# The last pair's expert results, summed by products with a matrix of weights at tokens instead of through memory

## The chip, the cores and the metric

The kernel runs on one core of a Trainium2 chip. The metric is the device time of one execution in microseconds (us); a time stated for a kernel is the median of its runs. The profile shows one execution, with its own time. Engines are named as in the profile: PE is TensorE (PEld its weight loads), DVE is VectorE, ACT is ScalarE, POOL is GpSimd, SP is SyncE, which here only issues DMAs.

## The reference, cut to what matters

A model of four layers on x, 4 x 256 tokens of 256 numbers, f32. Each layer adds an attention step and a feed-forward step to x. The change touches only the last one, a mixture of 64 experts of which each token uses 8:

```python
def _L3_ffn_ref(hidden_states, gate_w, gate_proj_w, up_proj_w, down_proj_w):
    B, S, H, I, E, K = (2, 128, 256, 96, 64, 8)      # run on the 1024 normed tokens
    x = hidden_states.reshape(-1, h)
    router_logits = x @ gate_w
    routing_weights, selected = jax.lax.top_k(router_logits, K)
    routing_weights = jax.nn.softmax(routing_weights, axis=-1)
    ...
    gate = jax.lax.ragged_dot(hidden_sorted, gate_proj_w, group_sizes)
    up = jax.lax.ragged_dot(hidden_sorted, up_proj_w, group_sizes)
    down = jax.lax.ragged_dot(jax.nn.silu(gate) * up, down_proj_w, group_sizes)
    out = down[unsort].reshape(-1, K, h)
    out = jnp.sum(out * routing_weights[..., None], axis=1)
...
x = x + _L3_ffn_ref(_layernorm(x, axis=-1), ...)
```

So each token's output is x plus a weighted sum of eight experts' results.

## The kernel before, in words

**Names.** P = 128 partitions, D = 256, NT = 8 tiles of 128 tokens (`x_t(t)` is tile t of x, kept on the chip), K3 = 8 choices of a token, E3 = 64 experts, CAP = 192 rows for each expert, S = 256. `ident` is the 128 x 128 identity, `kpos` holds 0 to 255 along each row. A token's eight choices are numbered in the order of their experts: choice 0 is its expert with the lowest number, choice 7 the one with the highest. `choice_w[:, t, j]` is the weight of choice j for the tokens of tile t.

**Scatter.** While the third layer's attention ends, GpSimd writes the normed row of each token eight times to `hs`, a buffer in HBM with 192 rows for each expert (L1702). Each row is HW = 257 wide; its last element is the number 8 * token + choice of the place where its result belongs. Rows that stay empty carry NPAIR = 8192 there, one beyond the end. `yd`, in HBM too, has a row for each of these 8192 places and is filled with zeros early in the kernel.

**The expert loop** (`experts`, L2040) takes two experts at a time, in 32 pairs, numbered 0 to 31. For a pair p, whose 384 rows stand in `hbs[p]` as three groups j of 128 rows: TensorE turns the rows (`rows_turned`, L1892), ScalarE copies them back (L1900), TensorE makes the gate sums (L2055) and the up sums (L1986), ScalarE the gate's silu (L2059), VectorE two products (L2071, L1991), TensorE the results of 384 rows (L1999, L2004), and ScalarE copies these over the pair's rows in `hbs[p]` (L2083). Then `put_results(p)` has GpSimd write them to `yd` by three indirect DMAs, one for each group of 128 rows (L2009), to the places that the rows carry. The iteration for pair p+1 does the results of pair p. At its end `beside(p)` places what else runs: the choice weights of a tile in even pairs below 16, two diagonal matrices a pair from pair 16 on (`diag[:, t // 2, j, :]` is `ident` times the weight of choice j, for the even tiles t; L2025), the rows of pair p + 7 (`load_rows`, L443), weights of later experts (L416), the loads of `load_results`, and four early adds (L1939).

The order on TensorE, VectorE, ScalarE, GpSimd and SyncE is the program's order (`tc.manual_schedule`): a waiting instruction holds up what stands behind it on its engine. Waits follow from what an instruction reads and writes; the loads of `load_results` wait for just those puts that can hold their choices (`needs`, L421).

**Loads of results.** Since choices stand in the order of experts, the rows of choice j are complete in `yd` after a certain pair. `LOADS` groups the choices (0 and 1, 2, 3, 4, 5, 6 and 7) and L1952 computes the pair: 23, 27, 28, 29, 30 and 31. `load_results(js, p)` (L1908, L1927) then loads these choices of all tokens back to the chip, 1 MB for a choice, in one DMA, in two halves, or for 6 and 7 in four parts, all on SyncE's queue; `result(t, j)` is the part for tile t.

**The sums** (`sums`, L2094) follow the last pair. For the even tiles TensorE adds up the choices in PSUM, by products of `diag` with `result` (`sum_result`, L1944), choice by choice over the four tiles: choices 0 to 5 first, then 6 and 7 tile by tile; VectorE adds x (L1779). For the odd tiles VectorE does all: x plus weight times result, one operation for each choice (`add_result`, L1939), behind a marker on GpSimd (`tick`, L2101) that stands after its last put. ScalarE's queue issues the eight stores (L2096).

## Time and profile before

| what | value |
|---|---|
| median of 10 runs | 642.79 us (642.0 to 644.01) |
| the profiled execution: time / span | 643.89 us / 642.2 us |
| busy PE / PEld / DVE / ACT / POOL, us | 590.6 / 449.9 / 423.9 / 373.8 / 403.3 |
| mean granted TensorE clock | 0.971 |
| chain that ended last, by engine | PE 44%; POOL 18%; issue 12%; DVE 10%; ACT 8%; DMA 5% |
| puts to `yd` (L2009) | x84 shown with hb as source, 1001 ns mean |
| sums on TensorE (L1944) | from 618.22 to 638.73 us of the span |

How to read it: times inside the execution are us from the start of its span, which is 1.7 us shorter than its time. A line of a table of stretches gives, for each engine, busy time and the number of instructions, then the granted clock (1.00 is full speed), the busy share of the DMA engines and GB/s. In a timeline a line has start, length, engine, line of the kernel, operation, output<-inputs and a count of records; what stands in brackets is idle time before it and what ended that. TensorE's matmuls are pipelined, so the distance from one to the next counts, not the length of a record. A few records can be missing from a trace.

### The profile page before, as it was taken

To read this page: it belongs to the slowest core of one execution; us is meant where nothing else is said; L and a number is where in the kernel's file an instruction comes from. 1 tells how busy PE (TensorE), PEld (TensorE's weight loads), DVE (VectorE), ACT (ScalarE), POOL (GpSimd) and SP (SyncE) were. 2 spreads that over 40 slices of the span, in tenths; PEclk is the share of its full clock that TensorE was granted. 3 is DMA by queue.
4 is the path that set the end of the run, shared out by engine and by line. 5 is a ranking of instruction groups with operands and counts; after the bars stand their busy time and mean duration, and the time that the engine had idled before them with its cause. 6 is when DMAs were issued, how large, how long until landed. Compare 5 with 4: busy or idle time off the path is not lost.

```text
span 642.2 us, 10891 instructions
## 1 busy us (share of the span) xinstructions
PE 590.6 (92%) x3727; PEld 449.9 (70%) x3740; DVE 423.9 (66%) x1063; ACT 373.8 (58%) x900; POOL 403.3 (63%) x532
## 2 busy tenths in 40 slices
PE   5997799998999999999999989999839999999995
PEld 4773347686688777877877867886627887778873
DVE  5678947878687789669988766485534555433437
ACT  2233337868988976456886768579444454545420
POOL 6997898213627543664735885787773777676660
PEclk9997979999999999999999989999959999999998
DMA  8999999920210023000003111053458978979687
GB/s 283 365 387 239 193 198 176 301 61 26 83 33 3 1 66 115 2 0 1 1 2 98 42 67 58 34 187 108 159 150 281 300 239 276 305 229 304 212 265 263
DMA packets 66305, 98.13 MB, mean 153 GB/s; under 512 B 7206, under 2 KB 54007, under 8 KB 66240
## 3 DMA queue, kind: packets, MB, share of 16 engines
q1 hardware_dynamic: 56320, 78.40, 43.0%
q0 software_dynamic: 7680, 16.84, 7.4%
q10 hardware_dynamic: 2240, 2.10, 1.0%
q8 instruction: 32, 0.52, 0.4%
q14 instruction: 33, 0.27, 0.1%
HBM read 58.42 MB, written 43.07 MB: 158 GB/s over the span
## 4 chain that ended last, share of the span: by engine, by line
PE 44%; POOL 18%; issue 12%; DVE 10%; ACT 8%; DMA 5%; POOLq 1%; SPq 1%; DVEq 0%; ACTq 0%
POOL yd L2009 10%; PE ps_q L1519 5%; PE ps_y L1623 3%; POOL hs L1702 3%; PE ps_g L1120 3%; PE ps_u L1120 2%; PE ps_y L1402 2%; DMA hs<-hx,slots 2%; PE ps_u L1604 2%; DMA hb<-hs 2%; PE ps_p L742 2%; PE ps_s L1380 2%; PE tp_q L1277 2%; PE ps_s L1554 1%; PE tp_e L1588 1%
## 5 line engine op out<-in xcount | busy, mean ns | idle before, releaser
L2009 POOL DMA_INDIRECT yd<-hb x84 | 84.1, 1001 | 34.2 <-issue 20.4
L1702 POOL DMA_INDIRECT hs<-hx,slots x64 | 65.7, 1026 | 24.2 <-issue 13.0
L903 POOL TENSOR_TENSOR st<-st,mhalf 128x1 f32<-128x1 f32 x56 | 33.0, 593 | 56.4 <-DVE st L899 44.2
L1566 ACT ACTIVATE e<-ps_s,nm 128x128 f32<-128x128 f32 x128 | 45.8, 412 | 5.6 <-DVE nm L1560 5.5
L1991 DVE TENSOR_TENSOR act<-ps_u,g 64x192 f32<-64x192 f32 x64 | 22.7, 354 | 39.7 <-PE ps_u L1986 39.3
L2083 ACT COPY hb<-ps_y 128x768 f32<-128x768 f32 x27 | 21.6, 800 | 36.5 <-PE ps_y L2004 36.5
L2071 DVE TENSOR_TENSOR act<-ps_gu,g 32x384 f32<-32x384 f32 x32 | 18.0, 562 | 33.8 <-ACT g L2059 33.5
L1478 POOL TENSOR_TENSOR hh<-g,v 128x512 f32<-128x512 f32 x16 | 20.2, 1274 | 23.8 <-ACT g L1476 19.9
L1281 ACT ACTIVATE qT<-tp_q,rnd 128x512 bf16<-128x512 f32 (+2 forms) x48 | 25.7, 567 | 10.8 <-PE tp_q L1277 10.7
L1566 ACT ACTIVATION_READ_ACCUMULATOR e<-ps_s,nm 128x1 f32 x128 | 31.2, 251 | 0.0
L1533 POOL TENSOR_TENSOR deep<-rt 64x512 f32<-64x512 f32 x20 | 27.0, 1348 | 5.9 <-DVE rt L1529 2.7
L1519 PE MATMUL ps_q<-qc,deep 96*128 96x256 f32 x128 | 30.4, 380 | 0.0
L1185 ACT ACTIVATE e<-ps_s,nb 128x256 f32<-128x256 f32 x64 | 30.1, 493 | 0.0
L906 DVE TENSOR_SCALAR h<-x,st 128x256 f32<-128x256 f32 x56 | 26.7, 488 | 5.1 <-POOL st L903 4.8
L1623 PE MATMUL ps_y<-bo,u 128*128 128x256 f32 x128 | 29.3, 381 | 0.1
L2059 ACT ACTIVATE g<-ps_gu 96x384 f32<-96x384 f32 x32 | 15.6, 486 | 23.2 <-PE ps_gu L2055 23.2
L1900 ACT COPY hbT<-tp_hb 128x768 f32<-128x768 f32 x31 | 24.7, 798 | 6.9 <-PE tp_hb L1892 5.1
L1120 PE MATMUL ps_g<-hT,w_gate 128*128 128x512 bf16 x69 | 21.0, 447 | 8.0 <-ACT hT L1100 4.3
L1529 DVE TENSOR_TENSOR rt<-ps_q,rope 128x512 f32<-128x512 f32 x32 | 20.9, 684 | 9.4 <-PE ps_q L1519 9.4
L1583 DVE TENSOR_TENSOR e<-e,nm 128x512 f32<-128x512 f32 x32 | 25.8, 806 | 1.3
L1519 PEld LDWEIGHTS ps_q<-qc,deep 96*128 96x128 f32 x128 | 24.1, 190 | 3.5 <-ACT qc L1505 0.3
L1623 PEld LDWEIGHTS ps_y<-bo,u 128*128 128x128 f32 x128 | 23.6, 190 | 3.4 <-ACT u L1608 0.5
(373 smaller groups left out, 1777.3 us busy)
## 6 DMA issues: line engine op xcount, KB each, us to landing
hs<-order SPq DMA_DIRECT2D x1, 12336.0 KB, 95.2
hb<-hs SPq DMA_DIRECT2D x28, 385.5 KB, 5.7
yd<-order SPq DMA_DIRECT2D x1, 8192.0 KB, 30.6
deep<-in_w_gu SPq DMA_DIRECT2D x8, 768.0 KB, 6.4
wt<-in_w_gu SPq DMA_DIRECT2D x6, 768.0 KB, 6.0
deep<-in_w_dn SPq DMA_DIRECT2D x8, 384.0 KB, 6.2
wt<-yd SPq DMA_DIRECT2D x3, 1024.0 KB, 7.3
wt<-in_w_dn SPq DMA_DIRECT2D x6, 384.0 KB, 8.5
```

The costliest lines, as they stand in the source:

```text
L903: nc.gpsimd.tensor_tensor(s[:, 8:9], s[:, 7:8], mhalf, ALU.pow)
L906: nc.vector.tensor_scalar(h[:, k, :], x_t(t), ss[k][:, 6:7], ss[k][:, 8:9], ALU.subtract, ALU.mult)
L1120: nc.tensor.matmul(ps.ap, w[:, dc, o : o + P], q[:, dc, :], start=k == 0, stop=k == n - 1)
L1185: nc.scalar.activation(e[:, mt, :], s[:, mt, :], AF.Exp, bias=nb[:, mt : mt + 1], accum_out=tot[:, 2 * j + mt : 2 * j + mt + 1],)
L1281: nc.scalar.activation(qT[:, 4 * i : 4 * i + full, :], tp.ap[:, :full, :], AF.Identity, bias=rnd[:, 1:2])
L1519: nc.tensor.matmul(ps.ap[:, k, :], w[:, hp * P : (hp + 1) * P], qc.ap, start=True, stop=True)
L1533: nc.gpsimd.tensor_add(qv(q[i])[r, hps, :], t0[r], t1[r])
L1566: nc.scalar.activation(wide[:, k, :], s.ap[:, k, :], AF.Exp, bias=nm[:, k : k + 1], accum_out=tot[:, k : k + 1],)
L1583: nc.vector.tensor_mul(wide, wide, tot.unsqueeze(2).to_broadcast([P, n, nk * P]))
L1623: nc.tensor.matmul(y.ap, u[:, hp, :], bo3[:, hp, :], start=hp == 0, stop=hp == H3 // 2 - 1)
L1702: put = nc.gpsimd.indirect_dma_start(out=hs[:, :], out_offset=bass.IndirectOffsetOnAxis(ap=slots[:, t, j : j + 1], axis=0), in_=rows[:, j, ...
L2009: put = nc.gpsimd.indirect_dma_start(out=yd[:, :], out_offset=bass.IndirectOffsetOnAxis(ap=hbs[p][:, j, D : D + 1].bitcast(I32), axis=0), ...
```

## The change

The rows of the last pair (31) are not written to `yd` any more. Each of the pair's three groups of 128 rows gets, for each of four blocks of 256 tokens, a matrix of 128 rows by 256 tokens that holds the row's weight in the column of its token and zero elsewhere (`own_part`, twelve in all, on old buffers and four new ones). In the sums TensorE multiplies these with the results that still stand in `hbs[31]`. In `yd` the places of these rows keep their zeros, so the other sums add nothing for them, and all choices can be loaded after pair 30 at the latest. Every tile, odd ones too, now has its own sum in PSUM, which starts with x (`sum_x`, a product with the identity) or with the last pair's part (`sum_own`). Choices 4 and 5 of odd tiles are scaled by ScalarE in place and added by products with the identity (`sum_scaled`); choices 0 to 3 of odd tiles are added to x by VectorE as before, choices 6 and 7 by VectorE on the sum. ScalarE copies the even tiles' sums to x; the odd tiles' stores go to SyncE's queue.

In the loop, `own_rows` (pair 2) loads the places that the last pair's rows carry; `own_tokens` (pair 15) works out the tokens and writes `choice_w` to a new HBM buffer `wd`; `own_weights` (pairs 16, 20, 24) gathers the rows' weights from it by an indirect DMA each; `own_places` (pairs 18 to 29, one matrix a pair) makes the matrices.

The diff, cut to its core:

```diff
+    wd = dram.tile([NPAIR, 1], F32, tag="wd", name="wd")
...
+    part_of = [moe_tile([P, S], f"own{k}", 1) for k in range(4)] + [dsc0, b2o]
+    part_of += [
+        q.bitcast(F32)[:, k * S : (k + 1) * S]
+        for q in (q12, q1_both.rearrange("p k i -> p (k i)")[:, : 2 * RPP * HW]) for k in range(RPP)
+    ]
+    own_i, own, own_w = (moe_tile([P, RPP], n, 1) for n in ("own_i", "own", "own_w"))
+    own_from = moe_tile([P, NT * P // S, RPP], "own_from", 1)
...
+    last = n_pairs - 1
+    def own_rows():
+        ld = nc.sync.dma_start(
+            own_i.bitcast(I32),
+            hs[2 * last * CAP :, D : D + 1].bitcast(I32).rearrange("(j p) o -> p (j o)", p=P),
+        )
+        needs(ld, "put", [i for js in puts for i in js], "rows of all choices")
+    def own_tokens():
+        nc.vector.tensor_copy(own, own_i.bitcast(I32))
+        nc.vector.tensor_scalar(own, own, 1.0 / K3, 0.5 / K3 - 0.5, ALU.mult, ALU.add)
+        nc.vector.tensor_scalar(own, own, ROUND, ROUND, ALU.add, ALU.subtract)
+        for k in range(NT * P // S):
+            nc.vector.tensor_scalar(own_from[:, k], own, float(k * S), None, ALU.subtract)
+        nc.vector.memset(own_w, 0.0)
+        nc.sync.dma_start(wd[:, :].rearrange("(t p j) o -> p t (j o)", p=P, j=K3), choice_w)
+    def own_weights(j):
+        nc.gpsimd.indirect_dma_start(
+            out=own_w[:, j : j + 1], out_offset=None, in_=wd[:, :],
+            in_offset=bass.IndirectOffsetOnAxis(ap=own_i[:, j : j + 1].bitcast(I32), axis=0),
+            bounds_check=NPAIR - 1, oob_is_err=False,
+        )
+    def own_part(j, k):
+        return part_of[j * (NT * P // S) + k]
+    def own_places(j, k):
+        nc.vector.tensor_scalar(
+            own_part(j, k), kpos, own_from[:, k, j : j + 1], own_w[:, j : j + 1], ALU.is_equal, ALU.mult
+        )
...
-            y, diag[:, t // 2, j, :], result(t, j), start=j == 0, stop=j == K3 - 1
+        nc.tensor.matmul(y, diag[:, t // 2, j, :], result(t, j), start=False, stop=j == K3 - 1)
+    def sum_x(y, t):
+        nc.tensor.matmul(y, ident, x_t(t), start=t % 2 == 0, stop=False)
+    def sum_scaled(y, t, j):
+        nc.tensor.matmul(y, ident, result(t, j), start=False, stop=j == K3 - 3)
+    def sum_own(y, t):
+        for j in (0, 2, 1):
+            k, o = divmod(t * P, S)
+            nc.tensor.matmul(
+                y, own_part(j, k)[:, o : o + P], hbs[last][:, j, :D], start=t % 2 == 1 and j == 0, stop=False
+            )
     for js in LOADS:
-        last = max(min(BOUND[j] - 1, E3 - K3 + j) // 2 for j in js)
-        loaded[last] = js
+        p = max(min(BOUND[j] - 1, E3 - K3 + j, E3 - 3) // 2 for j in js)
+        loaded.setdefault(p, []).append(js)
...
-        if p in loaded:
-            load_results(loaded[p], p)
+        for js in loaded.get(p, ()):
+            load_results(js, p)
+        if p == FIRST:
+            own_rows()
+        if p == 2 * NT - 1:
+            own_tokens()
+        if p in own_at:
+            own_weights(own_at[p])
+        if 0 <= p - own_first - 2 < RPP * NT * P // S:
+            own_places(*divmod(p - own_first - 2, NT * P // S))
         if p in added_at:
             add_result(*added_at[p])
+    own_first = 2 * NT
+    own_at = {own_first + j * NT * P // S: j for j in range(RPP)}
...
                     nc.scalar.copy(yb[:, 1, :], y[:, 1])
+                    beside(p - 1)
+                    break
                 put_results(p - 1, yb)
...
     def sums():
-        ys = {t: (ps_mm if t < NT // 2 else ps_acc)([P, D], "ps_sum") for t in range(0, NT, 2)}
+        first = [ps_mm([P, D], "ps_sum") for _ in range(2)]
+        second = [ps_acc([P, 4, D], "ps_sums") for _ in range(2)]
+        ys = (
+            first[0], tp_rows[:, 0, :D], first[1], tp_rows[:, 1, :D],
+            second[0][:, 0], second[0][:, 2], second[1][:, 0], second[1][:, 2],
+        )
+        evens, odds = range(0, NT, 2), range(1, NT, 2)
         put_out = nc.gpsimd.memset(tick, 0.0)
-        for j in range(K3 - 2):
-            for t in range(0, NT, 2):
+        for t, j in on_dve[EARLY_ADDS : -NT]:
+            if j < K3 - 4:
+                add = add_result(t, j)
...
+        def known_sums(t):
+            sum_x(ys[t], t)
+            for j in range(K3 - 4):
                 sum_result(ys[t], t, j)
-        for t, j in on_dve[EARLY_ADDS : -NT]:
-            add = add_result(t, j)
...
-        for t in range(0, NT, 2):
-            for j in range(K3 - 2, K3):
+        for t in evens[:-1]:
+            known_sums(t)
+        for t in range(NT - 2):
+            sum_own(ys[t], t)
+        known_sums(NT - 2)
+        for t in (NT - 2, NT - 1):
+            sum_own(ys[t], t)
+        for t in odds:
+            sum_x(ys[t], t)
+        for j in (K3 - 4, K3 - 3):
+            for t in odds:
+                nc.scalar.activation(
+                    result(t, j), result(t, j), AF.Copy, scale=choice_w[:, t, j : j + 1]
+                )
+            for t in evens:
                 sum_result(ys[t], t, j)
-                add_result(t + 1, j)
-            store(t + 1)
-            add_to_x(t, ys[t])
-            store(t)
+            for t in odds:
+                sum_scaled(ys[t], t, j)
+        for t in evens:
+            for j in (K3 - 2, K3 - 1):
+                sum_result(ys[t], t, j)
+            nc.scalar.copy(x_t(t), ys[t])
+            store(nc.scalar, t)
+            for j, v in ((K3 - 2, ys[t + 1]), (K3 - 1, x_t(t + 1))):
+                nc.vector.scalar_tensor_tensor(
+                    x_t(t + 1), result(t + 1, j), choice_w[:, t + 1, j : j + 1], v, ALU.mult, ALU.add
+                )
+            store(nc.sync, t + 1)
```

More of the change, by code (lines that the diff above doesn't have):

```diff
@@ L1943, in sum_result @@
     def sum_result(y, t, j):
-        nc.tensor.matmul(
-            y, diag[:, t // 2, j, :], result(t, j), start=j == 0, stop=j == K3 - 1
-        )
+        nc.tensor.matmul(y, diag[:, t // 2, j, :], result(t, j), start=False, stop=j == K3 - 1)
[9 more added lines that the diff above has]
+            )
     loaded = {}
     for js in LOADS:
-        last = max(min(BOUND[j] - 1, E3 - K3 + j) // 2 for j in js)
-        loaded[last] = js
+        p = max(min(BOUND[j] - 1, E3 - K3 + j, E3 - 3) // 2 for j in js)
+        loaded.setdefault(p, []).append(js)
     on_pe = [(t, j) for j in range(K3) for t in range(0, NT, 2)]
@@ L2094, in sums @@
     def sums():
-        def store(t):
-            nc.scalar.dma_start(out[t // 2, t % 2 * P : (t % 2 + 1) * P, :], x_t(t))
-        ys = {t: (ps_mm if t < NT // 2 else ps_acc)([P, D], "ps_sum") for t in range(0, NT, 2)}
-        put_out = nc.gpsimd.memset(tick, 0.0)
-        for j in range(K3 - 2):
-            for t in range(0, NT, 2):
-                sum_result(ys[t], t, j)
-        for t, j in on_dve[EARLY_ADDS : -NT]:
-            add = add_result(t, j)
-            tc.add_manual_dep(
-                add.ins, put_out.ins.name,
-                mybir.DependencyInfo(mybir.DependencyClass.Sync, mybir.DependencyReason.DATA),
-                reason="the last results are on their way",
-            )
@@ L2112, in sums, with store @@
-        for t in range(0, NT, 2):
-            for j in range(K3 - 2, K3):
-                sum_result(ys[t], t, j)
-                add_result(t + 1, j)
-            store(t + 1)
-            add_to_x(t, ys[t])
-            store(t)
+        def store(queue, t):
+            queue.dma_start(out[t // 2, t % 2 * P : (t % 2 + 1) * P, :], x_t(t))
+        first = [ps_mm([P, D], "ps_sum") for _ in range(2)]
[4 more added lines that the diff above has]
+        )
@@ new lines, in sums @@
+        evens, odds = range(0, NT, 2), range(1, NT, 2)
+        put_out = nc.gpsimd.memset(tick, 0.0)
+        for t, j in on_dve[EARLY_ADDS : -NT]:
+            if j < K3 - 4:
+                add = add_result(t, j)
+                tc.add_manual_dep(
+                    add.ins, put_out.ins.name,
+                    mybir.DependencyInfo(mybir.DependencyClass.Sync, mybir.DependencyReason.DATA),
+                    reason="the last results are on their way",
+                )
+        def known_sums(t):
+            sum_x(ys[t], t)
+            for j in range(K3 - 4):
+                sum_result(ys[t], t, j)
@@ L2120, in model @@
+        for t in evens:
[6 more added lines that the diff above has]
+                    x_t(t + 1), result(t + 1, j), choice_w[:, t + 1, j : j + 1], v, ALU.mult, ALU.add
+                )
+            store(nc.sync, t + 1)
     with tc.manual_schedule(engines=ORDERED | {mybir.EngineType.SP}):
```

## The prediction

> **What bounds the kernel now.** The change touches the expert loop and the sums behind it, so I first read the table of stretches (width, then busy time of each engine with its instructions, granted clock, DMA share, GB/s):

> ```profile
> core 0: us, PE busy (x) PEld busy (x) DVE busy (x) ACT busy (x) POOL busy (x), PEclk, DMA share, GB/s
> ...
> 580.00:600.00 20.00, 20.00 (x143) 15.69 (x141) 8.23 (x25) 9.82 (x15) 13.81 (x15) 1.00 0.82 268
> 600.00:610.00 10.00, 10.00 (x73) 8.24 (x72) 4.28 (x14) 4.87 (x8) 6.80 (x7) 1.00 0.59 211
> 610.00:620.00 10.00, 9.17 (x57) 6.42 (x56) 4.41 (x14) 3.84 (x6) 7.17 (x8) 1.00 0.72 214
> 620.00:630.00 10.00, 7.76 (x34) 6.21 (x34) 5.42 (x14) 0.00 (x0) 3.63 (x5) 0.98 0.95 314
> ```

> The loop is bound by TensorE (20.00 of 20.00 us); from 620 on TensorE idles and the DMA is full. Second, the chain that ended last, from 600 us on:

> ```profile
> 623.51 3.33 DMA yd<-hb
> ...
> 626.96 6.63 DMA cx<-yd
> ...
> 638.83 0.36 DVE x L1779
> ```

> The end hangs on the last pair's puts, on their landing, and on the load of choices 6 and 7 behind them. This is the chain that the change cuts. Third, what TensorE does meanwhile (start, length, line; xN are records):

> ```profile
> 618.22 1.13 PE L1944 MATMUL ps_sum<-deep,diag 128*128 128x256 f32 x4
> ...
> 620.92 4.48 PE L1944 MATMUL ps_sum<-wt,diag 128*128 128x256 f32 x20
> 625.23 1.03 PE L1944 MATMUL ps_sum<-q,diag 128*128 128x256 f32 x4
> 626.54 1.13 PE L1944 MATMUL ps_sum<-q,diag 128*128 128x256 f32 x4 [0.28 <-DMA q<-yd]
> 629.63 2.08 PE L1944 MATMUL ps_sum<-q,diag 128*128 128x256 f32 x4 [1.96 <-DMA q<-yd]
> ...
> 636.32 2.41 PE L1944 MATMUL ps_sum<-ctxT,diag 128*128 128x256 f32 x8 [0.21 <-DMA ctxT<-yd]
> ```

> The page for L1944 adds up to 64 records (24+12+8+8+8+4), and sum_result is called 32 times (8 choices, 4 even tiles): one f32 product of 128x128 by 128x256 is two records. From 620.92 to 625.23 stand 20 records, 10 products: **0.431 us a product**. The whole stage of 32 needs 13.8 us of TensorE and lies in a window of 20.5 us (618.22 to 638.73); 6.7 us are waits and low clock. That 6.7 us is all the cover there is for new products.

> **The change part by part.** The page's execution has a span of 642.2 us and a time of 643.89; the median of the ten runs is 642.79. I work out a difference of spans and add it to the median.

> 1. Products in the sums. By the diff: known_sums on four even tiles, 4 x (1 + 4) = 20; sum_own on eight tiles, 8 x 3 = 24; sum_x on four odd tiles, 4; choices 4 and 5, 2 x (4 + 4) = 16; choices 6 and 7 of the even tiles, 8. That is **72 products in place of 32**, all of the one shape, in one written order on TensorE. 72 x 0.431 = 31.0 us. Started at 618.22 like today and never waiting, they end at 649.25 instead of 638.73: +10.5 us. No row prices them lower: 379 ns is a record's length in the pipeline, 0.2155 us its pitch, and the slow rows are slower (0.81 us a product at half clock, the 1.62 us of weight loads for wmask). The cover of 6.7 us is counted in this difference already.

> 2. The new order makes a wait. Today choice 3 is first read by the 13th product (618.22 + 12 x 0.438 = 623.5). Now known_sums(0) reads it in the fifth, at 618.22 + 4 x 0.431 = 619.95. Its load, by the source line of the loads:

> ```profile
> L1927 SPq DMA_DIRECT2D wt<-yd x1: 360/360/360, 616.5 to 616.5; - x1
> ...
> DMA to landing us min/median/max: 5.8/5.8/5.8
> ```

> It is issued at 616.5, when pair 28's puts have landed, and lands at 622.3 in the full DMA stretch. The diff moves neither its pair (28) nor what runs beside it. TensorE waits from 619.95 to 622.3: **+2.35 us**, with all 68 other products queued behind it. Were it to land after the 4.0 us of this line's shortest load, at 620.5, the wait would be 0.5; after 9.2, the longest, 5.75. I take its own row.

> 3. The clock after that wait. Three stretches of 3.41 us, one on each side of the clock's fall and one with a smaller gap:

> ```profile
> 626.12:629.53 3.41, 1.27 (x5) 0.68 (x4) 3.41 (x10) 0.00 (x0) 0.00 (x0) 1.00 0.84 255
> 629.53:632.94 3.41, 3.31 (x8) 2.53 (x8) 3.06 (x8) 0.00 (x0) 0.00 (x0) 0.50 0.94 297
> 165.32:168.73 3.41, 2.08 (x15) 1.53 (x15) 2.37 (x7) 3.30 (x6) 3.24 (x5) 1.00 0.57 175
> ```

> With TensorE busy 1.27 of 3.41 us the clock falls to 0.50 for the next 3.41 us; with 2.08 of 3.41 it does not. A wait of 2.35 us inside one such stretch leaves 1.06 us busy, fewer than the 1.27 that fell. If the fall comes, half of 3.41 us is lost: **+1.7 us**. Whether the stretch contains the wait depends on where it begins. With the limit midway (1.7 us idle), the wait is split too evenly to matter in 1.05 of 3.41 positions; so about 7 in 10 that it falls (9 in 10 and 5 in 10 at the two ends of the bracket). I take the fall. [...]

> 4. After the products. Today 3.47 us lie between the last product's end (638.73) and the span's end: an add of 0.42, a store of 2.4 and the close. Now it is a copy on ScalarE (0.37, as L2088) and a store behind it: the same 3.5 us. ScalarE needs about 0.8 us for each tile (0.37 and an issue of 0.38, median), TensorE 0.86, so it keeps up; were each issue the longest shown, 0.93, it would end about 1 us later. VectorE's two operations for each odd tile (2 x 0.48) are done before the last even tile's.

> 5. Loads, puts, adds. Choices 6 and 7 are asked for behind choice 5, at about 625.6 instead of 626.96; 3 MB at the 330 to 390 GB/s of these stretches land by 634 to 636. TensorE reaches choice 5 after 60 products, beyond 645, and choice 6 later: no wait, and nothing gained, since TensorE is last. The three puts of pair 31 (3 x 1.28 us) go, off TensorE's path. VectorE's twelve adds start near 620.7 (behind the third put at 619.68) and need 5.5 us; sum_x of the odd tiles, product 45, comes after 640. The eight scalings on ScalarE (0.49 at most, from L1185) take 3.9 us between landing and use.

> 6. Inside the loop (4.255 us a pair). Twelve own_places, one a pair from 18 to 29: 0.488 us each by L906 (same size, two scalars per partition). VectorE idles 1.32 us before L2071 in these pairs, 0.92 where an early add stands: hidden, with 0.4 us or more left. Uncovered, 5.9 us. Eight small operations in pair 15 (8 x 0.154 by L899) meet 1.72 us of idle. Three gathers on POOL at the 1.28 us pitch of a put: POOL has 4.255 - 3 x 1.275 = 0.43 us free a pair, so each is worked off in three pairs, before the next, and the rows behind are loaded seven pairs ahead. own_rows and the write of wd go on SP's queue, which waits there for puts already. The one wait that can reach TensorE: own_places stands in VectorE's order before L2071, and waits for its gather. From the gather's issue (about 595.8 for the third, after the put at 594.54) to that place two pairs later (600.1, after the diag operations) are 4.3 us, plus 0.8 of idle. Indirect writes land in 2.3 to 6.7 us in these stretches; the first gather also waits for wd, whose 1024 rows of 32 bytes no row prices. Each may cost 0 to 1.6 us: 0 to 5 in all. I take 0, since the median landings at the first two places are 2.3 to 3.4. [...]

> Sum: 10.5 + 2.35 + 1.7 = 14.6 us; span about 656.8, median **657.4 us**.

> **The rivals.**
> (a) Faster: the two records of a product are not the pitch I take them for, and a product costs 0.2155 us. Then 68 of them end at 622.3 + 14.7 = 637.0, the shorter DMA chain (choices 6 and 7 1.3 us sooner) shows, and the median is about 641. It decides only where a product costs under 0.22 us. For it stands the chain, where the DMA is last; against it the 64 records for 32 calls. 3%; no measurable change, 1%.
> (b) No wait for choice 3 (it lands before 620): the products alone, 653.3. 8%.
> (c) The wait, but the clock stays: 655.7. 26%.
> (d) My forecast, wait and clock: 657.4. 44%.
> (e) The forecast and a loss in the loop, from the gathers or a VectorE operation not covered: 1 to 4 us, 658.4 to 661.4. 18%.

> **How the numbers follow.** A measurement of this kernel tells about 0.2% (1.3 us) from no change. Faster is (a), 3%; within it 1%; slower is the rest, 96%. The range reaches from just below (b) to most of (e): 653.0 to 660.8.

> **What would show it.** In the profile after: 144 records under the four lines of the sums in place of 64, back to back up to about 653; the last loads landed some 15 us before TensorE's end; a wait of about 2.3 us on wt<-yd near 620, and half clock in the 3.4 us behind it; TensorE, not POOL and DMA, on the chain's last 30 us; the loop's pairs still 4.255 us. I am wrong if products come closer than 0.43 us, if TensorE still idles behind 623, or if L2071 comes late in pairs 18, 22 and 26.

## The result, and the profile after

The changed kernel takes **657.82 us** (median of 13 runs, 655.22 to 661.77); the kernel before took 643.0 us (median of 46 runs) beside it. The ratio is 1.0234, with an interval of 1.022 to 1.0249: slower by 14.8 us. The profiled execution took 657.77 us, its span is 656.0 us; the span before was 642.2 us, so 13.8 us are to be found in the two traces. Line numbers below are those of the changed kernel.

The table of stretches comes first again (width; busy time of PE, PEld, DVE, ACT and POOL, each with its instructions; granted clock, DMA share, GB/s):

```profile
580.00:600.00 20.00, 19.14 (x133) 14.81 (x130) 9.33 (x28) 9.03 (x13) 15.06 (x16) 1.00 0.82 263
...
620.00:630.00 10.00, 8.11 (x38) 6.88 (x37) 4.84 (x12) 2.00 (x5) 1.04 (x2) 1.00 0.87 292
630.00:640.00 10.00, 10.00 (x48) 8.77 (x47) 0.00 (x0) 1.62 (x4) 0.00 (x0) 1.00 0.57 205
640.00:650.00 10.00, 10.00 (x48) 8.80 (x47) 1.84 (x4) 0.37 (x1) 0.00 (x0) 1.00 0.04 13
```

From 630 on TensorE is busy all the time at full clock and the DMA engines run empty (0.04 busy after 640). Before, in the same place, TensorE had waited for loads. Two other things are new: TensorE stands idle for 0.86 us in the loop (19.14 of 20.00, before it was 20.00; the pair there is 5.75 us long instead of 4.25), and no stretch of the sums up to 650 shows a lower clock.

The chain that ended last, from 600 us on, added up by engine and line, says the same:

```profile
by line: PE ps_sums L1986 10.8%; PE ps_sum L1986 10.5%; DMA wt<-yd 10.4%; PE ps_gu L2118 9.5%; PE ps_sums L1997 9.3%; PE ps_y L2052 7.0%; PE ps_u L2039 5.7%; PE ps_sum L1997 4.6%; PE tp_hb L1997 4.6%; PE tp_hb L1934 3.5%; PE ps_y L2057 3.5%
```

The puts (`yd<-hb`) and the loads of choices 6 and 7 (`cx<-yd`), which carried the end before, are gone from it. The products of the sums (L1986, L1997) and one load, that of choice 3 (`wt<-yd`), stand in their place. TensorE's timeline shows where that load enters:

```profile
618.32 0.70 PE L1989 MATMUL ps_sum<-x,ident 128*128 128x256 f32 x2
618.86 1.03 PE L1986 MATMUL ps_sum<-deep,diag 128*128 128x256 f32 x4
619.72 0.59 PE L1986 MATMUL ps_sum<-wt,diag 128*128 128x256 f32 x2
622.21 0.70 PE L1986 MATMUL ps_sum<-wt,diag 128*128 128x256 f32 x2 [1.89 <-DMA wt<-yd]
```

After x and choices 0 to 2 of the first tile (eight records, four products) the fifth product waits for choice 3. Behind it there is no other gap: 144 records stand under the four lines of the sums, and the last one starts at 651.45.

The waits of the loop and the sums together (engine, output, line, what it waited for; us in total, times, longest):

```profile
DVE dsc L1909 <- DMA own_w<-wd,own_i: 3.1, 1, 3.1
PEld ps_sum L1986 <- DMA wt<-yd: 2.3, 1, 2.3
DVE q L1909 <- DMA own_w<-wd,own_i: 2.0, 1, 2.0
DVE x L2209 <- ACT x L2206: 1.9, 1, 1.9
```

Two of the four are VectorE at `own_places` (L1909), waiting for the gathered weights (a third wait there is 0.4 us long); one is VectorE at the end, waiting for ScalarE. I had put both at nothing.

**Where the 13.8 us are.** The first silu of the loop starts at 479.32 instead of 481.27 (-1.95). From there to the first product of the sums it is 139.00 us instead of 136.95 (+2.05). From the first product to the span's end, which I call the stage of the sums, it is 37.68 instead of 23.98 (+13.70). The sum is +13.80.

### The profile page after: what moved, and what is told of

It reads as the page before. It is cut to its first block, busy times and chain, and to the rows that moved or that the text cites. A ratio compares the mean times of both kernels' runs of the same rounds, so it can differ in the third digit from the quotient of the medians.

```text
span 656.0 us, 11068 instructions
## 1 busy us (share of the span) xinstructions
PE 603.4 (92%) x3807; PEld 465.0 (71%) x3820; DVE 423.5 (65%) x1071; ACT 379.3 (58%) x912; POOL 406.3 (62%) x532
## 4 chain that ended last, share of the span: by engine, by line
PE 60%; DVE 12%; ACT 8%; POOL 7%; DMA 6%; issue 5%; POOLq 0%; SPq 0%; DVEq 0%; ACTq 0%
PE ps_gu L2118 6%; PE ps_q L1520 5%; PE ps_y L2052 3%; PE ps_u L2039 3%; PE tp_hb L1934 3%; PE ps_y L1624 3%; DMA hs<-hx,slots 2%; PE ps_u L1605 2%; POOL hs L1703 2%; PE ps_p L743 2%; PE ps_y L1403 2%; PE ps_u L1121 2%; PE ps_y L2057 2%; PE ps_s L1381 2%; PE tp_e L1589 2%
## 5 line engine op out<-in xcount | busy, mean ns | idle before, releaser
L2062 POOL DMA_INDIRECT yd<-hb x81 | 82.0, 1013 | 30.1 <-issue 20.4
L2134 DVE TENSOR_TENSOR act<-ps_gu,g 32x384 f32<-32x384 f32 x32 | 18.0, 561 | 27.0 <-ACT g L2122 26.7
L1121 PE MATMUL ps_g<-hT,w_gate 128*128 128x512 bf16 x69 | 18.3, 401 | 8.5 <-ACT hT L1101 4.5
```

Of the source, the lines that this page charges most:

```text
L1121: nc.tensor.matmul(ps.ap, w[:, dc, o : o + P], q[:, dc, :], start=k == 0, stop=k == n - 1)
L2062: put = nc.gpsimd.indirect_dma_start(out=yd[:, :], out_offset=bass.IndirectOffsetOnAxis(ap=hbs[p][:, j, D : D + 1].bitcast(I32), axis=0), ...
```

## The experiments

The theory: the 40 additional products cost their pitch in full, because nothing in the stage hides them; the wait for choice 3, the end, and the loop are small beside them. The rival: the products lie beside loads that TensorE would have waited for anyway, and the time comes from the new waits. A second question was whether the chain that the change cuts was worth anything. The first four kernels ran on one chip (the kernel before: 643.95 us there); cut_again and split2_again ran on another (643.07). The other six (loop_only, cut_only, mended, mended_again, split, split2) ran on a chip where the kernel before takes 675 to 676 us and the pairs of the loop are irregular, called the slower chip below, so of those six I read mainly the stage of the sums and the ratio to the kernel before on the same chip. Diffs are against the changed kernel unless said.

**The changed kernel once more**, unedited, beside the next three kernels on their chip.

> The changed kernel once more, for a second profile and as the measure of the others on the same chip. All theories: about 657.8 us, 72 products at 0.431 us in the sums, TensorE idle 1.9 to 2.4 us at the fifth product. They differ on the clock: if a wait of this length makes it fall in most executions, this profile shows 0.50 for 3.41 us behind the wait with 7 chances in 10; if a wait of 1.9 us is too short, since 1.5 of 3.41 us stay busy and the profile before fell at 1.27, the clock stays at 1.00 whatever the position.

657.92 us, ratio 1.0216 (1.0181 to 1.0252). The stage takes 36.9 us, with a wait of 1.23 us for choice 3. The loop lost 4.6 us here: pair 20 to 21 took 8.33 us and pair 28 to 29 4.76, where 4.25 is usual. VectorE's line at the first of these, and two stretches of 3.41 us around it:

```profile
567.43 0.41 DVE L1909 TENSOR_SCALAR own<-kpos,own_from,own_w 128x256 f32<-128x256 f32 x1 [4.26 <-DMA own_w<-wd,own_i]
```

```profile
565.15:568.56 3.41, 1.61 (x13) 0.83 (x12) 1.06 (x3) 0.28 (x1) 2.50 (x4) 1.00 1.03 304
568.56:571.97 3.41, 3.41 (x10) 2.68 (x11) 1.33 (x5) 0.80 (x1) 2.80 (x3) 0.51 0.78 258
```

The matrix waits 4.26 us for its gather, L2134 behind it comes late, TensorE runs dry, and in the next stretch the granted clock is 0.51. So a wait with a fall of the clock behind it, as I had forecast, does occur, but in the loop and not in the sums.

**late3**: choice 3 read late.

```diff
         def known_sums(t):
             sum_x(ys[t], t)
-            for j in range(K3 - 4):
+            for j in range(K3 - 5):
                 sum_result(ys[t], t, j)
...
+        for t in evens:
+            sum_result(ys[t], t, K3 - 5)
         for t in odds:
             sum_x(ys[t], t)
```

> Choice 3 of the even tiles is summed behind the last pair's products, before the odd tiles' sum_x; the number of products is the same 72. If the wait for choice 3's load stands on the path, TensorE runs from 618.3 without a stop and the time falls by 1.9 to 2.4 us against the changed kernel (about 655.6); if that wait also made the clock fall in 7 of 10 executions, by 3.1 us or more in the median (about 654.6). Rival, the wait is hidden or only moved to the next load: no change.

TensorE's timeline at the place of the wait:

```profile
617.34 0.59 PE L1986 MATMUL ps_sum<-wt,diag 128*128 128x256 f32 x2
617.77 0.59 PE L1989 MATMUL ps_sum<-x,ident 128*128 128x256 f32 x2
```

The gap is gone: 144 records from 615.94 to 646.91, 30.97 us for 72 products. The stage is 35.6 us, 1.3 less than in after_again, whose wait was 1.23. The median is 655.84 (ratio 1.0203, 1.0165 to 1.0241). That is 2.08 us below the unedited kernel, but the two intervals overlap: the profile shows that the wait is gone, the times alone do not show the gain.

**gathers**: the three gathers in pairs 16, 17 and 18 instead of 16, 20 and 24.

```diff
-    own_at = {own_first + j * NT * P // S: j for j in range(RPP)}
+    own_at = {own_first + j: j for j in range(RPP)}
```

> The three gathers of row weights stand in pairs 16, 17 and 18 in place of 16, 20 and 24; the matrices that use them stay in pairs 18 to 29, so the second and third gather get five and eight pairs in place of two. If own_places, waiting on them in VectorE's order, held up L2134 and TensorE by 1.5 and 0.2 us in the profile, both pairs become 4.25 us long and the time falls by 1.7 us (about 656.1). Rival, the gathers' own work on POOL and on the DMA queues is what costs: then moving them only moves the loss, 0 to 0.5 us.

The pairs that follow the second and third gather are back at 4.25 us; only pair 20 to 21, behind the first, is longer (5.25). So these loop losses are the gathers' landing; split2_again, with its gathers in the same three pairs, has no long pair behind any of them. The time did not show it: 657.98 us (1.0228, 1.0187 to 1.0269), since choice 3 landed late in this profile and the wait for it was 3.67 us, the stage 39.3. The wait falls on two stretches:

```profile
617.45:620.87 3.42, 1.74 (x8) 1.18 (x7) 0.00 (x0) 0.23 (x1) 2.60 (x3) 1.00 0.73 236
620.87:624.28 3.41, 1.59 (x7) 1.43 (x8) 3.00 (x8) 0.00 (x0) 0.38 (x2) 1.00 1.01 342
```

TensorE idles for 3.51 us in one piece, more than forecast, and the clock stays at 1.00. The wait is cut in two by a boundary of the stretches. That this is the reason is not shown: the second stretch keeps 1.59 us of work, and in after_again one with 1.61 was followed by 0.51.

**no_own**: the 24 products with the last pair's matrices left out (the results of experts 62 and 63 are then missing from the output).

```diff
-        for t in range(NT - 2):
-            sum_own(ys[t], t)
...
-        for t in (NT - 2, NT - 1):
-            sum_own(ys[t], t)
...
-        nc.tensor.matmul(y, ident, x_t(t), start=t % 2 == 0, stop=False)
+        nc.tensor.matmul(y, ident, x_t(t), start=True, stop=False)
```

> The 24 products with the last pair's results are left out, so the results of experts 62 and 63 are missing in the sum; all else stays. If the sums are bound by TensorE at 0.431 us a product, the time falls by 24 x 0.431 = 10.3 us (about 647.5). Rival, the loads of choices 5 to 7 or the additions on VectorE come last soon after: TensorE would then wait for them and the fall would be 5 us or less.

646.94 us, ratio 1.0054 (1.003 to 1.0078): 10.98 us below the unedited kernel, where 24 x 0.431 = 10.3 was expected. TensorE's row in the stretch that had been fed by loads before:

```profile
630.00:640.00 10.00, 10.00 (x48) 8.81 (x47) 1.84 (x4) 2.27 (x6) 0.00 (x0) 1.00 0.59 218
```

Even with a third of the products gone TensorE never idles there. This settles the main point against the rival: products cost their full pitch, and no wait takes the place of those left out. The loop's additions are all still in this kernel, and they cost what they cost in the changed one: from the first silu (478.81) to the first product (617.83) it is 139.02 us, against 136.95 before. That the first product comes no later than before (618.22) is due to a loop that began sooner.

**loop_only**: the kernel before, with the loop's additions (own_rows, own_tokens, own_weights, own_places) and nothing that uses them.

```diff
+        if p == FIRST:
+            own_rows()
+        if p == 2 * NT - 1:
+            own_tokens()
+        if p in own_at:
+            own_weights(own_at[p])
+        if 0 <= p - own_first - 2 < RPP * NT * P // S:
+            own_places(*divmod(p - own_first - 2, NT * P // S))
```

> The kernel before, with only the loop's part of the change: own_rows, own_tokens, the write of wd, the three gathers at pairs 16, 20 and 24 and the twelve matrices at pairs 18 to 29, which nothing uses. Puts, loads and sums are those of before. If the waits for gathers hold up TensorE as in the profiles of the changed kernel (pairs behind 18, 22 and 26 longer by 1.7 to 4.6 us together), the time rises by 1.7 to 4.6 us. Rival, the loop's part is hidden: no change, all pairs 4.25 us. It also tells whether the earlier start of the loop (first silu at 477.8 to 479.3 us in the changed kernels, 481.27 in the one profile of before) comes with the new tiles: then it starts before 479.5 here too; if 481.27 was one execution's chance, the next kernel, which has no new tile, shows it as well.

681.54 us, ratio 1.0111 (1.0076 to 1.0147), on the slower chip. There the loop waits for its row loads too, and pairs of 3.3 to 10 us stand beside each other in every kernel, so I cannot divide the 6.5 us between the additions and what the chip does to them. The trace does not place them in the loop either: one matrix waits for its gather, 1.1 us, the way from the first silu to the first product is 158.6 us against 158.3 in cut_only, which has no additions, and in the sums TensorE waits 5.8 us for loads. Taken with the 2.05 us in the changed kernel's own trace it says only that the additions can cost something.

**cut_only**: the kernel before with the chain cut and nothing else: pair 31's rows are not put (the results of experts 62 and 63 are missing), choices 6 and 7 are loaded after pair 30.

```diff
-        last = max(min(BOUND[j] - 1, E3 - K3 + j) // 2 for j in js)
-        loaded[last] = js
+        p = max(min(BOUND[j] - 1, E3 - K3 + j, E3 - 3) // 2 for j in js)
+        loaded.setdefault(p, []).append(js)
...
                     nc.scalar.copy(yb[:, 1, :], y[:, 1])
+                    beside(p - 1)
+                    break
                 put_results(p - 1, yb)
```

> The kernel before without pair 31's puts and with choices 6 and 7 loaded after pair 30; no product takes their place, so the results of experts 62 and 63 are missing. It shows what cutting the chain is worth with the 32 products of before. By the loads' issue (625.6 in place of 626.96, or sooner) the time falls by 1.3 to 4 us, to 639 to 642. Rival, the DMA is full from 618 on and the last load lands no sooner: no change.

675.11 us, ratio 1.0005 (0.9975 to 1.0034), on the slower chip. The stage is 20.5 us, but on that chip the loads stand differently to the loop's end, so I ran it again on one like the first:

> The kernel before without pair 31's puts, choices 6 and 7 loaded after pair 30, nothing in their place (the results of experts 62 and 63 are missing): once more, for a chip whose loop runs at 4.25 us a pair. It gives the most that the cut of the chain can bring. From the issue of the loads at 622.5 to 625.6 in place of 626.96, the last load lands by 634 to 636 in place of 637.6, so 1.3 to 4 us less than before; on the slower chip it was 0 in the whole (ratio 1.0005), with a sums stage of 20.5 us from first product to the span's end. Rival: 0 here too, because the DMA is full.

**642.88 us, ratio 0.9993 (0.9977 to 1.0009)**: the rival came, cutting the chain is worth nothing that the runs can tell (the interval leaves room for 1.5 us). Its own chain of waits begins to say why (start, length, what):

```profile
618.73 6.13 DMA yd<-hb
```

Before, the last put began at 623.51 and landed in 3.33 us, at 626.84. Here the last put is one of pair 30, it begins 4.78 us sooner at 618.73, and lands in 6.13 us, at 624.86. From its start to its landing the DMA engines are 0.94 busy, with the loads of choices 3 and 4 among others. But pair 30's last put was no quicker in the kernel before: it began at 619.68 and landed 5.77 us later, at 625.45. So the cut had only the 1.39 us from there to 626.84 to gain. SyncE's queue shows what became of them, first before, then here:

```profile
625.57 0.36 SPq L1927 DMA_DIRECT2D q<-yd  x1
625.98 0.51 SPq L1927 DMA_DIRECT2D wmask<-yd  x1
626.96 0.87 SPq L1927 DMA_DIRECT2D cx<-yd  x2
```

```profile
624.99 0.36 SPq L1927 DMA_DIRECT2D q<-yd  x1
625.40 0.51 SPq L1927 DMA_DIRECT2D wmask<-yd  x1
625.95 1.02 SPq L1927 DMA_DIRECT2D cx<-yd  x2
```

The two loads of choice 5 (`q`, `wmask`) wait for pair 30's puts too, and stand ahead of those of choices 6 and 7. Before, they had been issued when pair 31's last put landed, and the next load followed 0.12 us behind the landing; here it follows 1.09 us behind. That takes 0.97 of the 1.39 us, and the somewhat longer landing (6.13 against 5.77) another 0.36. The load of choices 6 and 7 starts 1.01 us sooner by the clock, but so does the whole stage: relative to the first product it starts 8.69 us behind it, against 8.74 before.

**mended**: three mends in one: late3; the gathers in pairs 16 to 18 with the matrices two pairs later (20 to 31); and the sums of an even tile and the odd tile behind it in different PSUM tiles.

```diff
-        if 0 <= p - own_first - 2 < RPP * NT * P // S:
-            own_places(*divmod(p - own_first - 2, NT * P // S))
+        if 0 <= p - own_first - 4 < RPP * NT * P // S:
+            own_places(*divmod(p - own_first - 4, NT * P // S))
...
-            second[0][:, 0], second[0][:, 2], second[1][:, 0], second[1][:, 2],
+            second[0][:, 0], second[1][:, 0], second[0][:, 2], second[1][:, 2],
```

> The changed kernel with its three side losses taken away: choice 3 summed late, gathers at pairs 16 to 18 with the matrices at 20 to 31, and the sums of odd tiles 5 and 7 in another PSUM tile than those of even tiles 4 and 6. All 72 products stay. Expected: no gap in the sums (2.05 us in the profile), every pair 4.25 us (1.7 to 4.6 us), the span ends 3.8 us after the last product's start in place of 4.57. Together 4.5 to 7 us, about 652.5. If the products are what the change costs, it stays 9 to 10 us above the kernel before. Rival, the waits are the main cost: it comes within 3 us of before.

> The mended kernel once more, since in the runs before both kernels took some 32 us more than in all earlier runs, on another chip. If its loop runs at 4.25 us a pair as in the first runs: no gap in the sums, every pair 4.25 us, the span ends 3.5 us after the last product's start, and the time is 652 to 653.5 us where the changed kernel takes 657.9: the products alone. Rival, the waits were most of the cost: within 3 us of the kernel before.

688.81 us (1.0213, 1.0183 to 1.0242) and 691.55 us (1.0237, 1.018 to 1.0294), both on the slower chip. That is 13.8 and 15.8 us above the kernel before, where 9 to 10 had been expected. The changed kernel itself was not run there, so what the mends bring in total stays open. The stage is 35.2 us in both, with no wait for choice 3, and no matrix waits for its gather. The end is answered by VectorE's timeline of the second one:

```profile
681.07 0.48 DVE L2211 SCALAR_TENSOR_TENSOR x<-cx,choice_w,x 128x256 f32<-128x256 f32 x1
681.48 0.47 DVE L2211 SCALAR_TENSOR_TENSOR x<-ctxT,choice_w,ps_sums 128x256 f32<-128x256 f32 x1
```

and the changed kernel's at the same two operations:

```profile
648.98 0.48 DVE L2209 SCALAR_TENSOR_TENSOR x<-cx,choice_w,x 128x256 f32<-128x256 f32 x1
651.41 0.48 DVE L2209 SCALAR_TENSOR_TENSOR x<-ctxT,choice_w,ps_sums 128x256 f32<-128x256 f32 x1 [1.94 <-ACT x L2206]
```

In the changed kernel the sums of tiles 4 and 5 are two parts of one PSUM tile, and VectorE's operation on tile 5 waits 1.94 us for ScalarE's copy of tile 4. With the two in different PSUM tiles it runs on without a gap, and the distance from the start of the last product's record to the span's end is 3.50 and 3.49 us instead of 4.57. Most of this gain is given back just ahead of it, as TensorE's timeline in mended shows:

```profile
680.48 1.13 PE L1986 MATMUL ps_sums<-ctxT,diag 128*128 128x256 f32 x4 [0.46 <-ACT x L2208]
```

Now the sums of tiles 4 and 6 share a PSUM tile, and TensorE's products for tile 6 wait for the same copy of tile 4. From the first product's start to the last one's it is 31.70 us instead of late3's 30.97, so the stage of 35.2 us is only some 0.4 us shorter than late3's 35.6.

**split**: less work on TensorE. The last pair's results are weighted while they leave PSUM and split into two bf16 parts whose sum replaces the f32 value; the matrices are 0 and 1 in bf16; VectorE adds choices 0 and 1 of all tiles in pairs 28 to 31. That leaves 28 f32 products and 48 bf16 ones; in split2_again's timeline a bf16 product takes 0.11 us, an f32 one 0.43. **split2** makes the two parts ahead of pair 31's side work and puts tile 6's sum in another PSUM tile than tile 4's.

```diff
     def own_places(j, k):
         nc.vector.tensor_scalar(
-            own_part(j, k), kpos, own_from[:, k, j : j + 1], own_w[:, j : j + 1], ALU.is_equal, ALU.mult
+            own_part(j, k), kpos, own_from[:, k, j : j + 1], None, ALU.is_equal
         )
...
-                    nc.scalar.copy(yb[:, 1, :], y[:, 1])
+                    for j in (0, 2, 1):
+                        w = own_w[:, j : j + 1]
+                        nc.scalar.activation(own_y[0][:, j, :], y[:, j], AF.Copy, scale=w)
+                        nc.vector.scalar_tensor_tensor(
+                            own_y[1][:, j, :], y[:, j], w, own_y[0][:, j, :], ALU.mult, ALU.subtract
+                        )
```

> The same idea with less work on TensorE: the last pair's results, times their weights, are held as two bf16 parts (high and rest), and the matrices as ones and zeros in bf16, so a tile and group cost two bf16 products in place of one f32; choices 0 and 1 of all tiles are added by VectorE in pairs 28 to 31; x and choices 2 to 7 of the even tiles on TensorE; odd tiles on VectorE as before, plus one addition of the last pair's sum each. TensorE then has 28 f32 products (12.1 us) and 48 bf16 products (about 5.5 us at 0.11 us each), to about 635.5 if it never waits; VectorE 32 operations of 0.41 us from 620.7 to 634. With the 3.8 us behind the last product: span 639, 3 us less than before. Rival, the loads bound it: 5 MB at 330 to 390 GB/s from 616.4 end at 631 to 634, and a late put moves that to 636; then the time equals that of the kernel before within 1 us.

> The split kernel with two waits taken away that its profile showed: the two bf16 parts are made before pair 31's side work on VectorE, and tile 6's sum lies in another PSUM tile than tile 4's. TensorE: 28 f32 and 48 bf16 products. If the loads land as in the first runs (choice 5 near 630, choices 6 and 7 by 635), the last product starts at about 635.5 and the span ends at 639, 3 us below before. Rival, pair 30's puts land only behind the loads of choices 3 and 4, as in split's profile, and the last load ends near 638: the time is that of before within 1.5 us.

> The second split kernel once more, for a chip whose loop runs at 4.25 us a pair. There its sums stage, 26.05 us on the slower chip with 5 us of waits for loads, should take 21 to 24 us (before: 23.95), so 0 to 3 us less than before unless the loop loses by the gathers. Rival: the loads still end last, and with the loop's losses of 1 to 2 us it comes out 0 to 3 us above before.

split: 681.55 us, 1.0118 (1.0082 to 1.0154), stage 29.5. split2: 680.14, 1.007 (1.0035 to 1.0104), stage 26.05. Both ran on the slower chip. split2_again, on one like the first: **644.82 us, 1.0023 (1.0002 to 1.0043)**, stage 26.4; the gathers hold up no pair there. With most of the added f32 work gone most of the loss is gone, which agrees with no_own, though split2 changes more than the products. The stage missed the 21 to 24 us that were expected, and the rival came. What is left is mainly waits for loads and the clock behind them:

```profile
633.08 2.07 PE L1988 MATMUL ps_sum<-q,diag 128*128 128x256 f32 x4 [0.87 <-DMA q<-yd]
```

TensorE waits for choices 4 and 5 again, as before the change, and behind the waits the granted clock is 0.50 from 632.92 to 636.33, as it was from 629.53 to 632.94 before. The last load lands at 639.76, before it was 637.55. None of the versions beats the kernel before.

## Why the prediction was right or wrong, point by point

The total came out within half a us (657.4 said, 657.82 measured), and the mechanism that carries it is shown: no_own takes products away and the time goes with them, and split2_again, which changes more at once, agrees. Three smaller terms were wrong, with opposite signs. The sum itself was made of spans: 14.6 us said, 13.8 us in the traces. The medians differ by 14.8 because the profiled execution before lay about 1 us above its median, so part of the closeness is chance.

- **Step 1, products** (+10.5): right, a little small. 72 products took 31.08 us (pitch 0.4317) against 20.13 us for the window before, so +10.95; in late3, 30.97. The window of 20.5 us had been read to the last record's end, the 31.0 us from pitch to pitch; a record's length, 0.38 us, is most of what was left out.
- **Step 2, the wait for choice 3** (+2.35): right in place and cause; 2.05 in the changed kernel's profile (landing near 622.2, 622.3 was said). From one execution to the next it moves: 1.23, 2.05 and 3.67 us in three profiles with the same order of the sums, 1.6 in no_own. All lie within the bracket of 0.5 to 5.75; the one row taken was no better than that.
- **Step 3, the clock after that wait** (+1.7, 7 in 10): wrong. None of the four profiles with this wait shows a fall behind it. Two of the waits (1.23 and 1.6 us) were shorter than my limit of 1.7 us idle, an estimate midway between two rows. In the other two (2.05 and 3.67 us) a stretch boundary lay inside the wait, a position to which I had given 3 in 10; two profiles are too few to say that it is more. The limit failed as well, on both sides. In gathers the second of the two stretches kept 1.59 us of work, less than the limit asks, and the clock stayed; in the changed kernel's profile a stretch with 1.84 us of work, more than it asks (143.61 to 147.03), was followed by 0.50. One of the chances was also miscounted: at the end of the bracket where 2.14 us idle are needed, the fall comes in 1.48 of 3.41 positions, 4 in 10 and not 5. Nor did the longer gap bring the fall: in after_again one of 1.80 us, in a stretch with 1.61 us of work, was followed by 0.51, and in gathers one of 3.51 us was followed by 1.00.
- **Step 4, the end** (3.5 us as today): wrong by +0.75 (4.57 against 3.82 from the last record's start). The sentence "VectorE's two operations for each odd tile are done before the last even tile's" counted durations and not what the operations wait for: two tiles share a PSUM tile, and VectorE stood for 1.94 us behind ScalarE's copy. mended shows it by undoing it (3.50), though its own arrangement makes TensorE wait instead.
- **Step 5, loads and puts** (0): right in its sum. The details differ: choice 4's load was issued at 622.49 instead of 618.60, and next to nothing moves after 640 while TensorE is busy to 651. The three puts taken away were worth nothing, but not only because TensorE is last: cut_again shows no measurable gain from them with the old sums either. The second view of the prediction, "the chain that the change cuts", was a true chain, but the 1.3 us by which rival (a) had the loads of choices 6 and 7 come sooner shrank to 0.05 us relative to the first product.
- **Step 6, the loop** (0, bounds 0 to 5): wrong, though within its bounds: +1.71 from two gathers in the changed kernel, 4.6 in after_again, 1.8 in no_own, 1.9 in late3. The operation itself was cheaper than said (0.404 us, not 0.488). The failing step is the landing: a gather issued at 595.71 let its matrix start at 602.00, and one issued at 578.87 let it start at 584.57, 5.7 to 6.3 us where I had taken the puts' medians of 2.3 to 3.4 and had 5.1 us of room. The first gather there, issued at 562.02, let its matrix start at 564.83, 2.8 us later, and one in after_again took 6.6 us to land, so the medians were possible values but no bound. The first gather also stands behind the write of `wd`, for which the prediction had no row: it took 6.7 us to land in the changed kernel's profile. L2134 (L2071 before) coming late behind a gather was one of the signs of being wrong that the prediction had named, and it came. The rest of the loop, +0.35 between pairs 0 and 1, has no cause that I tested.
- **Unforeseen**: the loop began 1.95 us sooner. In five profiles with the changed kernel's buffers it began at 477.8 to 479.3; two others began at 480.3 and 480.8, and before at 481.3. On the slower chip it began at 493.5, 495.0 and 495.7 with the changed kernel's buffers and at 495.2 with the old ones, so no difference shows there. The cause stays open.

Put together: steps 1 and 2 gave 13.0 us where 12.85 were said; step 3's 1.7 us did not come; the loop's +2.05 and the end's +0.75 were not in the sum, and the early start (-1.95) took most of them back. Of the rivals, (a) falls with the pitch of 0.4317, and cut_again does not show the gain that it counted on; (c) was right in that the clock stayed, (e) in its mechanism. The forecast's total was reached by a mixture of the two, and not by its own third step.

## What to carry to other kernels

A chain of waits says what ended last, not what it is worth to cut it: taking the last three puts away gave a ratio of 0.9993, because the put ahead of them landed only 1.39 us sooner, and other loads that waited for that same put stood ahead of the load that was to gain. Before work is moved to an engine that idles, count the idle time that the new order leaves, and not that of the old: 6.7 us of waits and low clock on TensorE did cover 6.7 us of products, and 72 f32 products of 0.43 us needed 31. And ask of each operation moved off the path what it reads: the two terms that I had set to nothing because the durations fitted (the matrices of the loop, the last tile's sum) both came from waits (for a gather, and for the copy of a sum that lay in the same PSUM tile), not from the work.
